# A graph-network layer on one Trainium2 core: ScalarE's PSUM seeds spread over its queue, a bias moved to GpSimd, layer-0 pieces reordered

## The chip, the cores and the metric

The kernel runs on one core of one Trainium2 chip. The metric is the device time of one execution in microseconds; the median of three runs counts.

## What is computed

There are 128 graphs of 64 nodes with 128 features each (`x`) and an adjacency matrix per graph (`adj`, zeros and ones, about one entry in eight set, the diagonal always). A message network runs on every pair of nodes, its output is masked by the adjacency and summed over the neighbours, and an update network adds to the node's features. Cut to what matters, the reference is:

```python
def mlp(x, w0, b0, g0, be0, w1, b1, g1, be1, w2, b2):
    h = layernorm(relu(x @ w0 + b0), g0, be0)
    h = layernorm(relu(h @ w1 + b1), g1, be1)
    return h @ w2 + b2

pair = concat([x_i, x_j])                    # for every i, j of a graph
messages = mlp(pair, msg_...) * adj[..., None]
agg = sum(messages, over j)
out = x + mlp(concat([x, agg]), upd_...)
```

## The kernel before

**Edges in slots.** The kernel does not run all 64 x 64 pairs. For each pair of graphs p (64 of them) it lays the set entries of the adjacency into 640 slots per graph and makes a selection matrix `s` from two halves: `i` (which row a slot belongs to, by way of `d`, `tp` and a cast) and `j` (which column, by a matmul `mk` against `posall` and a comparison with `cmpt`). The halves are written into `s` by DMAs from SyncE's queue. A gather by matmul, `rows` of the graph times `s`, then gives the first layer of the message network for every edge.

**Chunks.** A chunk is 512 slots, four tiles of 128. There are 160 chunks (NCHK), five for two pairs of graphs (QC = 5), ten for a block of four pairs (CPB = 10), 16 blocks. For chunk n the main loop does:

- `layer0(n)` (L553): the gather into one PSUM bank `hps`. A chunk meets one or two graphs' slots, so it is cut into pieces (L544); each piece is two matmuls, one with the low part `abl` of the rows and one with the high part `abh` (L559). ScalarE then writes `h`, relu with bias (L562).
- `stats0` (L564): four transposes into the bank `hT` (L568) and VectorE's statistics (L261), from which a standard deviation `m_sd` per edge follows on ScalarE (L269, `root_of`), once in five chunks.
- `seed(n)` (L595): before the second layer's matmuls are added into PSUM, the bank `z` of the chunk is filled with b1b times the standard deviation of each edge. VectorE does it in one instruction for the four tiles (L601), or ScalarE in four, one per tile, one after the other (L606). `by_vector` (L879) says which: chunks whose number ends in 3, 4 or 8 go to VectorE, the other seven of ten to ScalarE; in the first ten chunks also 1 and 5, and in the last eight every second one.
- `layer1(n)` (L609): eight matmul instructions, two for each tile, that add h times w1c onto the seeded bank (L614), then ScalarE's `y` (L617), and VectorE's statistics of `y` (`stats1`).

There are two `z` banks, for even and odd chunks; each is seeded anew once its last `y` has been read.

**Reductions and updates.** For each pair, GpSimd multiplies weights (L650) and TensorE reduces `y` to a sum per node (L665). For each block of four pairs the update network runs beside the chunks, one small stage at a time: `ysum`, transposes (L711), layers (L725), `layer_out` (L729) with VectorE, copies by ScalarE (L716). Its first bias is `bias0` (L696): m0 = c2u times the degree of a node plus ub0b, four instructions by VectorE for a block of four pairs (L699). The residual `xo` is GpSimd's (L705), as is the scaling `usdb` (L748).

**The order.** The schedule is written by hand. `at(n, place, fn, ...)` (L340) puts a call into a step and a place in it, and the main loop (L1034) goes through the steps n and, in each, through the places in this order: "a", "m", "s", then `layer1(n - L1)` with L1 = 8, then "b", `layer0(n)`, `stats0(n - 1)`, "k", `stats1(n - L1)`, "x", "x1", "x2", "e0", "e1", "e". Each engine runs its instructions in the order in which the program issues them. `seed(n)` is put at step n + L1 - 2, place "x": that is two steps ahead of the chunk's `layer1`, and on ScalarE behind `y` and `h` of that step. `bias0` is at place "m" of a block's step (L821); for the last block at place "e".

Of the kernel before, what the change touches and what calls it, by code (L numbers as in the profile page):

```python
# [14 lines left out]
ALU = mybir.AluOpType  # L15
# [9 lines left out]
def tile_gnn(  # L25
# [40 lines left out]
    nc = tc.nc  # L66
    B, N, C = x.shape
    P = 128
# [8 lines left out]
    CH = 4  # L77
    QC = QT // CH
    NCHK = NQ * QC
    PB = 4  # L80
    NB = NP // PB
    CPB = NCHK // NB
# [92 lines left out]
    W = {}  # L175
# [62 lines left out]
    def bc(t, n, axis=1):  # L238

        s = [P, n, C] if axis == 1 else [P, C, n]  # L240
        return t.unsqueeze(axis).to_broadcast(s)
# [60 lines left out]
    def edge_path(es):  # L302
# [37 lines left out]
        def at(n, place, fn, *args):  # L340
            plan.setdefault((n, place), []).append((fn, args))

        def run(n, place):
            for fn, args in plan.pop((n, place), ()):
                fn(*args)
# [198 lines left out]
        def pieces(n):  # L544

            at_, end = n * CH * P, (n + 1) * CH * P
            while at_ < end:
                g, e = divmod(at_, CAP)
                w = min(end - at_, CAP - e)
                yield g, e, at_ - n * CH * P, w  # L550
                at_ += w

        def layer0(n):  # L553

            ps = ps_h.tile([P, CH * P], F32, name="hps")
            for g, e, c, w in pieces(n):
                s = S[g // 2][:, g % 2, e:e + w]
                for k, ab in enumerate(blocks[g // (2 * PB)]["ab", g // 4 % 2]):
                    nc.tensor.matmul(ps[:, c:c + w], lhsT=ab[:, g % 4, :], rhs=s,  # L559
                                     start=(k == 0), stop=(k == 1))  # L560
            H[n] = hp.tile([P, CH * P], F32, name="h")
            nc.scalar.activation(H[n], ps, AF.Relu, bias=b0c)  # L562

        def stats0(n):  # L564
            q, c = divmod(n, QC)
            ps = ps_t.tile([P, CH, P], F32, name="hT")
            for t in range(CH):
                nc.tensor.transpose(ps[:, t, :], H[n][:, t * P:(t + 1) * P], ident)  # L568
            if c == 0:
                ST0[q] = stp.tile([P, QT // 2, 6], F32, name="st0", bufs=6)  # L570
            for t in range(0, CH, 2):
                two_stats(ST0[q][:, (CH * c + t) // 2, :], ps[:, t:t + 2, :])
# [12 lines left out]
        def z_of(n):  # L585

            if n not in Z:
                Z[n] = zbank(n % 2).rearrange("p (t c) -> p t c", t=CH)
            return Z[n]
# [2 lines left out]
            nc.tensor.matmul(z_of(n), lhsT=slot[:, 0:P], rhs=cmpt[:, 0:CH * C], start=True,  # L592
                             stop=True, skip_group_check=True)

        def seed(n):  # L595

            q, c = divmod(n, QC)
            z = z_of(n)
            k = CH * c
            if by_vector(n):  # L600
                nc.vector.tensor_tensor(  # L601
                    z, bc(W["b1b"], CH),
                    SR[q][:, k:k + CH].unsqueeze(2).to_broadcast([P, CH, C]), op=ALU.mult)
                return
            for t in range(CH):
                nc.scalar.activation(z[:, t, :], W["b1b"], AF.Copy,  # L606
                                     scale=SR[q][:, k + t:k + t + 1])

        def layer1(n):  # L609

            ps = Z.pop(n)
            h = H.pop(n)
            for t in range(CH):
                nc.tensor.matmul(ps[:, t, :], lhsT=h[:, t * P:(t + 1) * P], rhs=W["w1c"],  # L614
                                 start=False, stop=True, skip_group_check=True)
            Y[n] = yp.tile([P, CH, C], F32, name="y")
            nc.scalar.activation(Y[n], ps, AF.Relu)  # L617

        def stats1(n):
            q, c = divmod(n, QC)  # L620
            if c == 0:
                ST1[q] = stp.tile([P, QT // 2, 6], F32, name="st1", bufs=2)
            for t in range(0, CH, 2):
                two_stats(ST1[q][:, (CH * c + t) // 2, :], Y[n][:, t:t + 2, :])
# [58 lines left out]
        def wide(name, u):  # L683

            if name not in u.blk:
                u.blk[name] = updp.tile([P, PB, C], F32, name=name,
                                        bufs=2 if name in ("uo", "xo", "m0") else 1)
            return u.blk[name][:, u.q, :]
# [6 lines left out]

        def bias0(u):  # L696
            u.m0 = wide("m0", u)
            for q in range(u.n):
                nc.vector.scalar_tensor_tensor(  # L699
                    u.m0[:, q, :], W["c2u"], u.blk["deg"][:, u.k0 + q:u.k0 + q + 1], W["ub0b"],  # L700
                    op0=ALU.mult, op1=ALU.add)

        def residual(u):
            u.xo = wide("xo", u)
# [73 lines left out]
        L1 = QC + 3  # L778
# [29 lines left out]
        for b in reversed(range(NB)):  # L808
            o = b * CPB
            n = o + QC + SC  # L810

            if b < NB - 1:
                t = STEADY if b < NB - 3 else LAST[b - NB + 3]
# [6 lines left out]
            for u, n, t, m0_at, xo_at in units:  # L820
                at(n + m0_at, "e" if b == NB - 1 else "m", bias0, u)  # L821
                at(n + xo_at, "e", residual, u)
                at(n + t[0], "a", sums_out, u)
                at(n + t[1], "x", turn, u, "ysum")
                at(n + t[2], "a", turn_out, u, "ysum")
                at(n + t[3], "x", lambda u: layer(u, ("xn", u0a), ("ysumT", W["w2u"])), u)
                at(n + t[4], "m", layer_out, u, "uh", "m0")
                at(n + t[4], "e", upd_m0, u)
                at(n + t[5], "x", turn, u, "uh")
                at(n + t[6], "a", turn_out, u, "uh")  # L830
                at(n + t[7], "a", upd_root0, u)
                if t is STEADY:
                    at(n + t[7], "e", upd_shift, u, 0, PB)
                else:
                    for q0 in range(0, u.n, 2):
                        at(n + t[7], "x", upd_shift, u, q0, q0 + 2)
                at(n + t[8], "x", lambda u: layer(u, ("uhT", W["u1c"])), u)
                at(n + t[9], "m", layer_out, u, "uy", "usdb")
                at(n + t[9], "e", upd_m1, u)
                at(n + t[10], "x", turn, u, "uy")  # L840
                at(n + t[11], "a", turn_out, u, "uy")
                at(n + t[12], "a", upd_root1, u)
                at(n + t[12], "m", upd_inverse, u)
                at(n + t[13], "x", lambda u: layer(u, ("uyT", W["u2c"])), u)
                at(n + t[14], "e" if b == NB - 3 else "m", finish, u)
        for p in range(NP):
            n = p * TG * 2 // CH
# [10 lines left out]
            w = p // 2 * QC + QC + L1 + p % 2  # L858
            last = p // 2 == NQ - 1
            at(w - 4, "a", node_marks, p)  # L860
            q, h = divmod(p, 2)
# [5 lines left out]
        for q in range(NQ):  # L867
            n = q * QC + QC if q else LEAD
# [10 lines left out]
        def by_vector(n):  # L879
            if n >= NCHK - L1:  # L880
                return n % 2 == 1
            return n % CPB in (3, 4, 8) or (n < CPB and n % CPB in (1, 5))

        for n in range(2):
            at(L1 - 1 - n, "s", prime, n)
            at(L1 - 1, "x", seed, n)
        for n in range(2, NCHK):
            at(n + L1 - 2, "x", seed, n)

        warm = ps_y.tile([P, PB, C], F32, name="ys")  # L890

# [50 lines left out]
        compare_here(0, 0)  # L942
        distance(1)
        layer0(0)
        keep_busy(4)
        compare_here(0, 1)
        make_tp(1)
        distance(2)
        marks_here(1)
        layer0(1)  # L950
        keep_busy(4)
        rows_hi(0, 0, 2, 4)
        rows_here(1, 0)
        rows_here(1, 1)
        compare_here(1, 0)
        rows_lo(0, 0, 2, 4)
        layer0(2)
        keep_busy(2)
        make_tp(2)
# [75 lines left out]
        for n in range(last + 1):  # L1035
            run(n, "a")
            run(n, "m")
            if n == NCHK:
                stats0(n - 1)
            run(n, "s")  # L1040
            if 0 <= n - L1 < NCHK:
                layer1(n - L1)
            run(n, "b")
            if n + LEAD < QC or QC <= n < NCHK:
                layer0(n if n >= QC else n + LEAD)
            if n + 1 < QC or QC <= n - 1 < NCHK - 1:
                stats0(n - 1 if n > QC else n + 1)
            run(n, "k")
            if 0 <= n - L1 < NCHK:
                stats1(n - L1)  # L1050
            for k in ("x", "x1", "x2", "e0", "e1", "e"):
                run(n, k)
# [3 lines left out]
    with ExitStack() as es:  # L1056
        es.enter_context(tc.manual_schedule())
        flag = edge_path(es)
# [160 lines left out]
```

## Time and profile before

| | |
|---|---|
| time, median of three runs | 544.2 us (544.17 to 547.51) |
| the profiled execution's own time | 544.21 us |
| its span | 542.4 us |
| granted TensorE clock, mean | 0.996 |
| HBM read and written | 6.82 MB and 4.19 MB |
| L614 on TensorE | 1280 instructions, 280 ns mean |
| L606 on ScalarE, the seeds | 436 instructions, 372 ns mean |
| L601 on VectorE, the seeds | 51 instructions, 682 ns mean |
| L699 on VectorE, the first bias | 64 instructions, 496 ns mean (331 to 886) |
| L705 and L748 on GpSimd, 128 x 512 | 1285 and 1042 ns mean |

How to read it: the span is the time between the first and the last instruction of the profiled execution, and the run's time is 1.8 us more. PE is TensorE's matmuls, PEld its weight loads, DVE is VectorE, ACT ScalarE, POOL GpSimd, and SP SyncE, from whose queue the DMAs start. A line of the order in time has the start, the duration of the merged instructions, the engine, the line of the kernel, the operation, what is written from what, the shape and the count, and in brackets an idle time before it with what ended it. A line of a window has its bounds and length, then the busy time of PE, PEld, DVE, ACT and POOL with the number of instructions, the granted clock, the DMA share and GB/s.

### The profile page before, as it was taken

To read this page: it belongs to the slowest core of one execution; us is meant where nothing else is said; L and a number is where in the kernel's file an instruction comes from. 1 tells how busy PE (TensorE), PEld (TensorE's weight loads), DVE (VectorE), ACT (ScalarE), POOL (GpSimd) and SP (SyncE) were. 2 spreads that over 40 slices of the span, in tenths; PEclk is the share of its full clock that TensorE was granted. 3 is DMA by queue.
4 is the path that set the end of the run, shared out by engine and by line. 5 is a ranking of instruction groups with operands and counts; after the bars stand their busy time and mean duration, and the time that the engine had idled before them with its cause. 6 is when DMAs were issued, how large, how long until landed. Compare 5 with 4: busy or idle time off the path is not lost. (4 is left out here: it accounts for less than half of the span.)

```text
span 542.4 us, 15157 instructions
## 1 busy us (share of the span) xinstructions
PE 520.0 (96%) x5513; PEld 471.6 (87%) x5513; DVE 472.3 (87%) x1271; ACT 475.0 (88%) x1108; POOL 207.4 (38%) x419
## 2 busy tenths in 40 slices
PE   8989999999999999999999999999999999999784
PEld 7777889899898989989898989989999998988764
DVE  6759798998989899898989989898989989896745
ACT  6788999998989999898999989899999989887824
POOL 3103253525334363533435353443536254323230
PEclk9999999999999999999999999999999999999998
DMA  4456666545575665547464554557466445542101
GB/s 99 106 134 117 154 110 149 124 115 121 121 164 101 154 109 128 130 101 166 113 148 96 148 136 98 145 122 147 103 149 129 119 110 117 142 99 32 39 22 43
DMA packets 90762, 63.18 MB, mean 116 GB/s; under 512 B 57398, under 2 KB 74812, under 8 KB 90684
## 3 DMA queue, kind: packets, MB, share of 16 engines
q1 hardware_dynamic: 90396, 62.03, 51.3%
q8 instruction: 46, 0.75, 0.6%
q14 instruction: 32, 0.26, 0.1%
q10 hardware_dynamic: 288, 0.13, 0.1%
HBM read 6.82 MB, written 4.19 MB: 20 GB/s over the span
## 5 line engine op out<-in xcount | busy, mean ns | idle before, releaser
L614 PE MATMUL z<-w1c,h 128*128 128x128 f32 x1280 | 175.8, 280 | 5.2 <-DVE z L601 2.5
L614 PEld LDWEIGHTS z<-w1c,h 128*128 128x128 f32 x1280 | 155.6, 191 | 18.8 <-DVE z L601 8.6
L606 ACT ACTIVATE z<-b1b,m_sd 128x128 f32<-128x128 f32 x436 | 162.1, 372 | 10.7
L261 DVE BATCH_NORM_STATS2 st<-hT 128x6 f32<-128x256 f32 x320 | 118.8, 412 | 20.5 <-PE hT L568 18.3
L261 DVE BATCH_NORM_STATS2 st<-y 128x6 f32<-128x256 f32 x320 | 120.7, 418 | 4.2 <-ACT y L617 4.2
L617 ACT ACTIVATE y<-z 128x512 f32<-128x512 f32 x160 | 94.8, 593 | 20.6 <-PE z L614 19.1
L562 ACT ACTIVATE h<-hps,b0c 128x512 f32<-128x512 f32 x160 | 109.6, 685 | 3.2 <-PE hps L559 3.2
L568 PE MATMUL hT<-ident,h 128*128 128x128 f32 x640 | 97.5, 275 | 2.4 <-DVE st L261 1.3
L559 PE MATMUL hps<-s,abl 128*128 128x512 f32 (+3 forms) x256 | 91.9, 371 | 0.5 <-ACT s L926 0.4
L568 PEld LDWEIGHTS hT<-ident,h 128*128 128x128 f32 x640 | 73.7, 141 | 19.4 <-PE z L614 7.7
L650 POOL TENSOR_TENSOR w<-oh,m_q 128x192 f32<-128x192 f16 x126 | 61.5, 510 | 59.9 <-PE ma L711 25.9
L559 PE MATMUL hps<-s,abh 128*128 128x512 f32 (+3 forms) x256 | 78.0, 323 | 0.0
L517 POOL CAST i<-tp 128x640 fp32r<-128x640 f16 x58 | 41.7, 719 | 93.3 <-issue 47.9
L541 DVE TENSOR_TENSOR j<-mk,cmpt 128x320 fp32r<-128x320 f32 x124 | 58.5, 472 | 1.0 <-PE mk L533 1.0
L502 ACT ACTIVATE d<-slot,mid 128x640 f16<-128x640 f16 x64 | 52.8, 825 | 0.0
L559 PEld LDWEIGHTS hps<-s,abl 128*128 128x128 f32 x256 | 48.9, 191 | 3.6 <-ACT w2cT L200 2.0
L559 PEld LDWEIGHTS hps<-s,abh 128*128 128x128 f32 x256 | 48.9, 191 | 0.1
L665 PE MATMUL ys<-y,w 128*32 128x128 f32 x1488 | 47.0, 275 | 0.0
L665 PEld LDWEIGHTS ys<-y,w 128*32 128x32 f32 x1488 | 38.7, 110 | 4.1 <-issue 3.3
L493 DVE TENSOR_TENSOR abl<-mu,abh 128x512 fp32r<-128x512 f32 (+1 forms) x32 | 21.3, 664 | 22.9 <-ACT abh L487 22.9
L533 PE MATMUL mk<-tp,posall 128*128 128x320 f16 x126 | 37.7, 299 | 0.0
L279 POOL TENSOR_TENSOR m_v<-m_v,st 128x20 f32<-128x20 f32 x31 | 7.7, 250 | 78.3 <-DVE st L261 74.7
(204 smaller groups left out, 841.9 us busy)
## 6 DMA issues: line engine op xcount, KB each, us to landing
s<-i SPq DMA_DIRECT2D x124, 160.0 KB, 2.9
s<-j SPq DMA_DIRECT2D x124, 160.0 KB, 2.7
xn<-in_x_dram SPq DMA_DIRECT2D x15, 256.0 KB, 3.6
out_dram<-uo SPq DMA_DIRECT2D x15, 256.0 KB, 2.9
an<-in_adj_dram SPq DMA_DIRECT2D x16, 128.0 KB, 2.5
oh<-tp SPq DMA_TRANSPOSE x64, 3.3
xn<-in_x_dram SPq DMA_DIRECT2D x2, 128.0 KB
out_dram<-uo SPq DMA_DIRECT2D x2, 128.0 KB, 3.0
```

What stands on the lines that cost most here:

```text
L261: nc.vector.bn_stats(st, src.rearrange("p t c -> p c t"))
L502: nc.scalar.activation(D[p], slot, AF.Abs, bias=blocks[b]["mid"][:, q:q + 1], scale=-1.0)
L517: nc.gpsimd.tensor_copy(IR[p], TP[p])
L541: nc.vector.tensor_tensor(JR[p][:, c], MK.pop((p, k))[:, 0:HC], cmpt[:, c], op=ALU.is_equal)
L559: nc.tensor.matmul(ps[:, c:c + w], lhsT=ab[:, g % 4, :], rhs=s, start=(k == 0), stop=(k == 1))
L562: nc.scalar.activation(H[n], ps, AF.Relu, bias=b0c)
L568: nc.tensor.transpose(ps[:, t, :], H[n][:, t * P:(t + 1) * P], ident)
L606: nc.scalar.activation(z[:, t, :], W["b1b"], AF.Copy, scale=SR[q][:, k + t:k + t + 1])
L614: nc.tensor.matmul(ps[:, t, :], lhsT=h[:, t * P:(t + 1) * P], rhs=W["w1c"], start=False, stop=True, skip_group_check=True)
L617: nc.scalar.activation(Y[n], ps, AF.Relu)
L650: (nc.vector if p == NP - 2 else nc.gpsimd).tensor_tensor(WT[p][:, g], oh, qs, op=ALU.mult)
L665: nc.tensor.matmul(YS[b][g * N + m * HN:g * N + (m + 1) * HN, k, :], lhsT=w[:, g, m, u, :], rhs=y, start=(u == 0), stop=(u == TH - 1), til ...
```

## The change

Four edits. `layer0` runs a chunk's pieces with the widest first. `seed` takes the tiles that it is to write: with none it is VectorE's one instruction, else ScalarE's for those tiles. `by_vector` leaves chunks ending in 4 to ScalarE, so that it has eight of ten. And ScalarE's four seeds of a chunk are put in four places: tile 0 in the new place "y1" of step i = n + L1 - 2, tile 1 in "x" of step i, tile 2 in "y0" and tile 3 in "y2" of step i + 1. The new places run between `layer1` and `layer0` of a step, after "b". Chunk 0 and the last eight chunks keep the four together in "x". `bias0` becomes a multiply and an add by GpSimd over the whole block, in the places where VectorE's four stood.

```diff
         def layer0(n):
             ps = ps_h.tile([P, CH * P], F32, name="hps")
-            for g, e, c, w in pieces(n):
+            for g, e, c, w in sorted(pieces(n), key=lambda v: -v[3]):
...
-        def seed(n):
+        def seed(n, *tiles):
             q, c = divmod(n, QC)
             z = z_of(n)
             k = CH * c
-            if by_vector(n):
+            if not tiles:
                 nc.vector.tensor_tensor(
                     z, bc(W["b1b"], CH),
                     SR[q][:, k:k + CH].unsqueeze(2).to_broadcast([P, CH, C]), op=ALU.mult)
-                return
-            for t in range(CH):
+            for t in tiles:
                 nc.scalar.activation(z[:, t, :], W["b1b"], AF.Copy,
                                      scale=SR[q][:, k + t:k + t + 1])
...
         def bias0(u):
             u.m0 = wide("m0", u)
-            for q in range(u.n):
-                nc.vector.scalar_tensor_tensor(
-                    u.m0[:, q, :], W["c2u"], u.blk["deg"][:, u.k0 + q:u.k0 + q + 1], W["ub0b"],
-                    op0=ALU.mult, op1=ALU.add)
+            deg = u.blk["deg"][:, u.q].unsqueeze(2).to_broadcast([P, u.n, C])
+            nc.gpsimd.tensor_tensor(u.m0, bc(W["c2u"], u.n), deg, op=ALU.mult)
+            nc.gpsimd.tensor_tensor(u.m0, u.m0, bc(W["ub0b"], u.n), op=ALU.add)
...
-            return n % CPB in (3, 4, 8) or (n < CPB and n % CPB in (1, 5))
-
-        for n in range(2):
-            at(L1 - 1 - n, "s", prime, n)
-            at(L1 - 1, "x", seed, n)
-        for n in range(2, NCHK):
-            at(n + L1 - 2, "x", seed, n)
+            return n % CPB in (3, 8) or (n < CPB and n % CPB in (1, 5))
+
+        for n in range(NCHK):
+            if n < 2:
+                at(L1 - 1 - n, "s", prime, n)
+            i = max(n + L1 - 2, L1 - 1)
+            if by_vector(n):
+                at(i, "x", seed, n)
+            elif n >= NCHK - L1 or n == 0:
+                at(i, "x", seed, n, *range(CH))
+            else:
+                at(i, "y1", seed, n, 0)
+                at(i, "x", seed, n, 1)
+                at(i + 1, "y0", seed, n, 2)
+                at(i + 1, "y2", seed, n, 3)
...
             if 0 <= n - L1 < NCHK:
                 layer1(n - L1)
-            run(n, "b")
+            for k in ("b", "y0", "y1", "y2"):
+                run(n, k)
             if n + LEAD < QC or QC <= n < NCHK:
                 layer0(n if n >= QC else n + LEAD)
```

## The prediction

> **What bounds the kernel now.** I read the busy shares first, then the window of the steady part, then the order of time on TensorE and on ScalarE.
>
> ```profile
> PE 520.0 (96%) x5513; PEld 471.6 (87%) x5513; DVE 472.3 (87%) x1271; ACT 475.0 (88%) x1108; POOL 207.4 (38%) x419
> ...
> 90.08:464.31 374.23, 373.57 (x4058) 342.15 (x4057) 346.47 (x923) 347.40 (x807) 161.32 (x312) 1.00 0.57 128
> ```
>
> The second line is the window of chunks 20 to 139, twelve groups of ten: 374.23/12 = 31.19 us a group. TensorE is busy 373.57 of 374.23, VectorE and ScalarE 93%, GpSimd 43%. A chunk's step runs from its first `z` matmul (L614) to the next chunk's. In one group the TensorE lines read:
>
> ```profile
> 313.19 1.16 PE L614 MATMUL z<-w1c,h 128*128 128x128 f32 x8
> ...
> 315.09 1.06 PE L614 MATMUL z<-w1c,h 128*128 128x128 f32 x8
> ...
> 317.07 0.60 PE L711 MATMUL ma<-ident,uh 128*128 128x128 f32 x4
> 317.65 1.16 PE L614 MATMUL z<-w1c,h 128*128 128x128 f32 x8
> ...
> 320.68 1.06 PE L614 MATMUL z<-w1c,h 128*128 128x128 f32 x8
> ...
> 322.62 1.05 PE L614 MATMUL z<-w1c,h 128*128 128x128 f32 x8
> ...
> 327.43 1.16 PE L614 MATMUL z<-w1c,h 128*128 128x128 f32 x8
> ...
> 329.76 0.50 PE L614 MATMUL z<-w1c,h 128*128 128x128 f32 x3
> ```
>
> Named by the last digit of the chunk whose `z` opens them, the steps last: 0: 4.69, 1: 1.90, 2: 2.56, 3: 3.03, 4: 1.94, 5: 4.81, 6: 2.33, 7: 2.70, 8: 3.93, 9: 3.27 us. They are uneven because the reductions and the update's layers sit in some of them. **TensorE's order of work is the bound, and little of the group is waiting.** I find four stops: `z` at 317.65 (four transposes at 0.109 from 317.07 end their issue at 317.51: 0.14), `z` at 301.30 (0.13), and `hT` at 300.12 and 324.26 (0.16 and 0.21 beyond the gap that the same pair of instructions has elsewhere), the first two behind VectorE's seed, the others behind its statistics. A `z` that was waited for also loses 0.10 in its first matmul (0.377 for 0.275). Together 0.14 + 0.13 + 0.16 + 0.21 + 0.20 = 0.84 us of 31.19. No relief of another engine can give more than that.
>
> Now ScalarE in the same place:
>
> ```profile
> 318.84 0.60 ACT L617 ACTIVATE y<-z 128x512 f32<-128x512 f32 x1 [0.55 <-PE z L614]
> ...
> 320.12 1.59 ACT L606 ACTIVATE z<-b1b,m_sd 128x128 f32<-128x128 f32 x4
> 321.78 0.60 ACT L617 ACTIVATE y<-z 128x512 f32<-128x512 f32 x1
> 322.27 0.68 ACT L562 ACTIVATE h<-hps,b0c 128x512 f32<-128x512 f32 x1
> 322.84 1.59 ACT L606 ACTIVATE z<-b1b,m_sd 128x128 f32<-128x128 f32 x4
> ...
> 502.80 1.27 ACT L752 ACTIVATE usdb<-bu1b,um_sd 128x128 f32<-128x128 f32 x4
> ```
>
> The reader is to see two things. First, the seeds at 320.12 stand in step 3 and are chunk 5's: they end at 321.71, and `z` of chunk 5 starts at 322.62, 0.91 later. Those at 322.84, chunk 6's, end 3.0 ahead of 327.43. So seeds are ready well ahead of their `z`. Second, four seeds take 1.59 us. One lasts 0.372, so the distance between them is (1.59 - 0.372)/3 = 0.406: each waits for the one before it to end. The four `usdb` writes, the same instruction into SBUF, take 1.27, a distance of 0.29. [...]
>
> [...] all stops at `z` lie on the first of a chunk's eight matmuls. [...] here L508 lasts 347 to 1112 ns, the long ones beside GpSimd work.
>
> **Part 1, the seeds.** Before, all four of chunk n stood behind `h`, two steps ahead of its `z`. After, tile 0 stands behind `y` and tile 1 behind `h` of that step, and tiles 2 and 3 stand behind the `y` of the next step, which is the last one before their `z`. This makes a loop through TensorE that was not there: `z` of chunk c, `y` of c, the last seeds of c+1, `z` of c+1.
>
> Its length where ScalarE is free: `z` start to `y` start 1.10 (320.68 to 321.78); `y` to the next start 0.48 to 0.49; three seeds (tile 2 of c+1, tile 0 of c+2, tile 3 of c+1) start 0.29 apart, 0.58; the last one 0.37; release to the first matmul 0.06. Sum 2.59. Where chunk c+2 is VectorE's, the middle seed is missing and tile 3 waits for tile 2: 0.405 in place of 0.58. The steps in which c+1 is ScalarE's and TensorE's own work is shorter:
> - step 4: 2.59 for 1.94, +0.65.
> - step 1: `y` starts 1.20 behind `z` (313.19 to 314.39, four small instructions ahead of it); 1.20 + 0.48 + 0.405 + 0.37 + 0.06 = 2.52 for 1.90, +0.62.
> - step 6: an `abh` copy at +0.12, then 0.48 + 0.47 + 0.20, so `y` at 1.27; 2.59 for 2.33, +0.26.
> - step 3 comes to about 2.82 (`m_sd` adds 0.21) of 2.93 and just fits; steps 0, 5, 8 and 9 have room; chunks 3 and 8 are VectorE's.
>
> +1.53, and 3 x 0.10 for first matmuls that waited, +0.30. In step 7 `h` now ends about 3.4 us behind `z`, where the next layer 0 wants its bank at 3.3: +0.15. Sum +1.98 a group.
>
> What it gives: eight chunks at 4 x 0.29 take 9.3 us of ScalarE's queue where seven at 1.53 (322.84 to the next start at 324.37) took 10.7, -1.4 a group. VectorE loses one seed, -0.68 (L601). Neither is the bound, so both count only through the four stops: I take all of them as gone, -0.84.
>
> **Part 2, the first bias.** VectorE loses four L699 (1.82 us of its queue a group). GpSimd gets a multiply like L748 (1.04) and an add like L705 (1.29): 2.33 us a group. They come where GpSimd idled or waited for statistics, and push `m_v` and `posall` back by at most 2.3; `m_v` is wanted two steps on, `posall` at the first mark of step 7, some 3 us later. `m0` is wanted four steps later. So 0; without that cover, 2.3 a group at most. [...] Below zero it gives only what the stops already hold.
>
> **Part 3, the larger piece first.** Only chunks with a 128 and a 384 piece in that order change, two steps a group. In the present order the four matmuls run 318.56 to 319.22, 0.66; a chunk with the large piece first takes 0.61. -0.10 a group; bounds 0 and -0.2.
>
> **Sum.** 1.98 - 0.84 - 0.10 = +1.04 a group, x12 = 12.5. Chunks 10 to 19 (steps of 1.89, 2.05 and 2.34) +1.3; 140 to 149 (1.89, 1.94, 1.90) +1.9; 0 to 9, where VectorE is the bound (19.9 of 20 us from 40 to 60) and loses 0.68 of work against three or four short steps, +0.5. The last eight chunks are seeded as before, and the end after 496 keeps its chain: 0. In all +16.2. The profiled execution is 544.21 (span 542.4 and 1.8 around it), the median 544.2: 560.
>
> **Rivals.**
> - *Each `z` matmul waits for its own tile only* (faster). The fourth tile's matmuls start 0.61 behind the first, so the loop shrinks to about 1.98 and 1.91, just at the shortest steps; it decides below 1.94. Then only -0.94 a group stands: 14 groups, 531. Against it: the bank-wide waits above. 0.09.
> - *The loop is shorter than I reckon*, by 0.3 to 0.4 (seeds closer, `y` earlier): +0.8 in place of +1.98, 0 net: 541 to 548. For it: 0.29 is from SBUF writes. 0.09.
> - *The seeds still stand 0.41 apart, [...]* The first adds 0.23 in step 4, 0.1 in step 3 and late `h`, the second gives back 0.84: +0.5 to 0.85 a group, 567 to 572. 0.20.
> - *Likeliest*, as summed, its own range 551 to 567: 0.62.
>
> A measurement of this kernel can tell about 1% from no change. Faster 0.09, within 1% 0.09, slower 0.82. The range 546 to 574 leaves out the first rival, most of the second and a little at the top, some 0.18.
>
> **What would show it.** The profile after should have steps 4 and 1 at about 2.6 and 2.5 us for 1.94 and 1.90, step 6 near 2.6, and all others as they were or 0.1 shorter; idle of TensorE before L614 put down to ScalarE's `z`, more than 15 us in all; ScalarE and VectorE busy shares lower; L699 gone from VectorE and 2.33 us a group on GpSimd. If steps 1 and 4 stay below 2.1, I am wrong on the loop; if steps 3, 8 or 0 grow, another wait has come.

## The result, and the profile after

The changed kernel takes 560.48 us, the median of four runs (560.23 to 562.53), against 544.22 for the kernel before on the same chip (four runs). The ratio is 1.0292, 95% interval 1.0247 to 1.0337: slower, by 16.3 us. The profiled execution took 562.5 us with a span of 560.4. It is some 2 us longer than the other three, and its first `z` is 2 us later than in the profile before (36.47 for 34.48). These 2 us have nothing to do with the change: they are there at the first layer 0 already (11.34 for 9.28), and in this profile TensorE's full clock is on record from 10.65 us on, for 6.12 before (the same matmul, L473, takes 0.48 us at 9.97 here and 0.32 at 8.21 there). They are left out below.

Line numbers after: seeds L605, `z` L613, `y` L616, first bias L698 and L699. The busy shares:

```profile
PE 525.0 (94%) x5513; PEld 475.8 (85%) x5513; DVE 458.9 (82%) x1192; ACT 470.4 (84%) x1168; POOL 240.2 (43%) x453
```

and the window of chunks 20 to 139, columns as before:

```profile
94.36:481.99 387.63, 375.45 (x4056) 344.74 (x4057) 337.49 (x862) 342.24 (x854) 184.90 (x336) 1.00 0.55 123
```

A group of ten takes 387.63/12 = 32.30 us for 31.19. TensorE's busy time rose by 1.9 us, but the window by 13.4: TensorE, idle for 0.7 us of the window before (374.23 less 373.57), is now idle for 12.2. VectorE and ScalarE are both less busy than before. So none of the engines has become the bound; the order of work between two of them has. The list of waits says which (the columns are: waiting engine, tile and line, releaser, us in all, times, longest):

```profile
PEld z L613 <- ACT z L605: 31.7, 53, 0.9
...
PE z L613 <- ACT z L605: 17.8, 37, 1.1
```

PEld is TensorE's weight loads, which overlap the matmuls (together they are busy for 525.3 us, the matmuls alone for 525.0), so the two lines are not to be added. Before, they came to 4.2 us in 16 waits and 2.5 in 4. The same group of ten as in the prediction, TensorE in order of time:

```profile
325.23 1.16 PE L613 MATMUL z<-w1c,h 128*128 128x128 f32 x8
...
327.75 1.16 PE L613 MATMUL z<-w1c,h 128*128 128x128 f32 x8 [0.45 <-ACT z L605]
...
330.22 1.06 PE L613 MATMUL z<-w1c,h 128*128 128x128 f32 x8
...
333.12 1.12 PE L613 MATMUL z<-w1c,h 128*128 128x128 f32 x8
...
335.77 1.16 PE L613 MATMUL z<-w1c,h 128*128 128x128 f32 x8 [0.46 <-ACT z L605]
...
340.45 1.16 PE L613 MATMUL z<-w1c,h 128*128 128x128 f32 x8
...
343.04 1.16 PE L613 MATMUL z<-w1c,h 128*128 128x128 f32 x8
```

These lines open steps 1 to 7. Steps 1, 4 and 6 last 2.52, 2.65 and 2.59, and the `z` that closes them has the 1.16 us of a `z` that was waited for. Means over twelve groups, in us:

| step | 0 | 1 | 2 | 3 | 4 | 5 | 6 | 7 | 8 | 9 | sum |
|---|---|---|---|---|---|---|---|---|---|---|---|
| before | 4.70 | 1.90 | 2.57 | 3.04 | 1.95 | 4.81 | 2.33 | 2.69 | 3.93 | 3.27 | 31.19 |
| after | 4.71 | 2.51 | 2.48 | 2.91 | 2.63 | 4.69 | 2.59 | 2.47 | 4.04 | 3.27 | 32.30 |

The prediction's lengths of the steps before are up to 0.01 off these means and add up to 31.16, which changes nothing in its sum. What closes step 4 is read on ScalarE:

```profile
334.28 0.60 ACT L616 ACTIVATE y<-z 128x512 f32<-128x512 f32 x1 [0.38 <-PE z L613]
334.77 0.94 ACT L605 ACTIVATE z<-b1b,m_sd 128x128 f32<-128x128 f32 x3
335.65 0.67 ACT L562 ACTIVATE h<-hps,b0c 128x512 f32<-128x512 f32 x1
...
345.83 0.67 ACT L562 ACTIVATE h<-hps,b0c 128x512 f32<-128x512 f32 x1
```

`z` of step 4 starts at 333.12, `y` 1.16 later; 0.49 on, three seeds take 0.94 to 335.71; at 335.77 the next `z` starts. That is the loop, link by link, and ScalarE has waited 0.38 for `y`'s input inside it: each engine waits for the other once a turn. The three seeds start 0.29 apart (334.77, 335.06, 335.35), not 0.406: they go to alternating banks, and in this profile two seeds in a row start 0.29 apart in all 174 pairs that go to different `z` banks, 0.39 to 0.41 in the 47 pairs that go to one. No seed passes the `y` it stands behind: ScalarE's 1167 instructions start in the program's order without exception, as do VectorE's 1185 and GpSimd's 435. The last line belongs to step 8: this `h` ends at 346.50, and layer 0, which writes the bank that it reads, starts behind it at 346.55.

### The profile page after: what moved, and what is told of

It reads as the page before. It is cut to its first block, busy times and chain, and to the rows that moved or that the text cites. A ratio compares the mean times of both kernels' runs of the same rounds, so it can differ in the third digit from the quotient of the medians.

```text
span 560.4 us, 15158 instructions
## 1 busy us (share of the span) xinstructions
PE 525.0 (94%) x5513; PEld 475.8 (85%) x5513; DVE 458.9 (82%) x1192; ACT 470.4 (84%) x1168; POOL 240.2 (43%) x453
## 5 line engine op out<-in xcount | busy, mean ns | idle before, releaser
L613 PE MATMUL z<-w1c,h 128*128 128x128 f32 x1280 | 178.4, 282 | 20.9 <-ACT z L605 17.8
L613 PEld LDWEIGHTS z<-w1c,h 128*128 128x128 f32 x1280 | 155.1, 191 | 40.5 <-ACT z L605 31.7
L605 ACT ACTIVATE z<-b1b,m_sd 128x128 f32<-128x128 f32 x496 | 169.1, 368 | 2.7
L261 DVE BATCH_NORM_STATS2 st<-hT 128x6 f32<-128x256 f32 x320 | 120.5, 418 | 34.6 <-PE hT L568 33.4
L616 ACT ACTIVATE y<-z 128x512 f32<-128x512 f32 x160 | 95.1, 594 | 27.8 <-PE z L613 27.3
L562 ACT ACTIVATE h<-hps,b0c 128x512 f32<-128x512 f32 x160 | 108.0, 675 | 5.1 <-PE hps L559 5.0
L559 PE MATMUL hps<-s,abh 128*128 128x512 f32 (+3 forms) x256 | 74.6, 322 | 0.0
L487 ACT CAST abh<-mu 128x512 fp32r<-128x512 f32 (+1 forms) x32 | 18.3, 572 | 32.3 <-PE mu L475 32.3
```

The costliest lines, as they stand in the source:

```text
L261: nc.vector.bn_stats(st, src.rearrange("p t c -> p c t"))
L605: nc.scalar.activation(z[:, t, :], W["b1b"], AF.Copy, scale=SR[q][:, k + t:k + t + 1])
```

## The experiments

Ratios are to the kernel before on the same chip, whose medians were 544.3 to 545.4.

**Seeds of a chunk together again, the rest of the change kept.** In `after`:

```diff
-                at(i, "y1", seed, n, 0)
-                at(i, "x", seed, n, 1)
-                at(i + 1, "y0", seed, n, 2)
-                at(i + 1, "y2", seed, n, 3)
+                at(i, "x", seed, n, *range(CH))
```

> The changed kernel without the spread: the four seeds of a chunk together behind h, two steps ahead, as before; bias on GpSimd, eight chunks of ten on ScalarE and the larger piece first stay. Loop theory: no loop; but ScalarE's queue holds 8 x 1.53 + 18.2 = 30.4 us in a group of about 30.3 to 31.2, so it is nearly full and little is gained: 538 to 548 us. Rival (the other edits make the loss): 552 to 562 us.

539.63 us, ratio 0.9898 (0.9870 to 0.9926). Steps 4.71, 1.90, 2.57, 3.02, 1.94, 4.61, 2.45, 2.37, 3.87, 3.27, together 30.71. So everything in the change but the spread makes the kernel faster by 1%, and the spread costs 560.5 - 539.6 = 20.9 us.

**The spread alone.** In `before`, `seed(n, *tiles)` and the new places as in the change; chunks, bias and piece order as they were.

> The kernel before with the spread alone: VectorE keeps chunks 3, 4 and 8 and the bias, and the pieces keep their order. Loop theory: the three short steps stay at 2.5 to 2.6 us, since chunks 2, 5 and 7 are ScalarE's here too; VectorE's old stops may stay in part: 558 to 572 us, 562 most likely. Rival (the other edits make the loss): 540 to 548 us.

561.09 us, 1.0313 (1.0285 to 1.0340). Steps 4.71, 2.51, 2.48, 2.93, 2.58, 4.69, 2.59, 2.47, 4.07, 3.27, together 32.31 for 32.30 in `after`. The spread makes the whole of the loss by itself. The relief of VectorE, which gains 4 to 6 us where the seeds are together (the bias and the chunk each alone, below), gains 0.6 beside the spread: TensorE waits for ScalarE, and the step lengths are the same to 0.05 with it and without.

**The dose: the last two seeds behind `h` rather than behind `y`.** In `after`:

```diff
-                at(i + 1, "y0", seed, n, 2)
-                at(i + 1, "y2", seed, n, 3)
+                at(i + 1, "x", seed, n, 2)
+                at(i + 1, "x", seed, n, 3)
```

> The changed kernel with tiles 2 and 3 of each spread seed later still: behind h of the step ahead of their z, one after the other. Loop theory, from the same durations: z to y 1.10, y to its end 0.63 (tile 0 of the next chunk but one waits for it), 0.29, h 0.57, 0.40 between the two tiles, 0.37, 0.06: 3.42 us, 2.98 where the next chunk but one is VectorE's. Steps 4, 1, 6, 3 and 9 of a group become about 3.4, 3.1, 3.15, 3.6 and 3.4 us, +3.9 us a group against the kernel before: 592 to 608 us, 600 most likely. Rival (the loss is not in the loop but in the number of instructions or in contention): 555 to 566 us, as the changed kernel.

604.57 us, 1.1099 (1.1070 to 1.1128). Steps 1, 3, 4, 6 and 9 take 3.09, 3.63, 3.52, 3.17 and 3.42; a group 35.08. The waits grow with the links:

```profile
PEld z L613 <- ACT z L605: 78.2, 79, 1.7
PE z L613 <- ACT z L605: 60.8, 67, 1.4
```

**Late tiles and early tiles exchanged.** If each matmul waited for its own tile, late tiles 2 and 3 would cost less than late tiles 0 and 1, whose matmuls come first. In `after`:

```diff
-                at(i, "y1", seed, n, 0)
-                at(i, "x", seed, n, 1)
-                at(i + 1, "y0", seed, n, 2)
-                at(i + 1, "y2", seed, n, 3)
+                at(i, "y1", seed, n, 2)
+                at(i, "x", seed, n, 3)
+                at(i + 1, "y0", seed, n, 0)
+                at(i + 1, "y2", seed, n, 1)
```

> The changed kernel with the tiles' parts exchanged: tiles 2 and 3 are seeded early, tiles 0 and 1 are the late ones. If TensorE's first matmul on a bank waits for the whole bank (the prediction): the same as the changed kernel, 558 to 563 us. If each tile's matmuls wait for that tile's seed alone, the late tiles are now those that are needed first, some 0.4 us earlier in each of three steps, so 1.2 us a group more: 575 to 580 us.

560.39 us, 1.0290 (1.0268 to 1.0311): to 0.1 us the changed kernel.

```profile
PEld z L613 <- ACT z L605: 31.8, 53, 0.9
```

The same 53 waits and 31.8 for 31.7 us. The first matmul waits for the last seed of the bank, whichever tile it is for. In the traces this wait is one for a semaphore, which the program sets and asks for: in `after` all 125 waits of L613 for ScalarE's stand on the first of a chunk's eight matmuls, and all seeds but one (495 of 496) wait for ScalarE's own. So it is the program that guards the bank as a whole. No run leaves these waits out, so what the bank itself would hold up is not shown.

**The last two seeds ahead of the next `y`.** This takes them out of the loop and leaves them spread. In `after`:

```diff
-                at(i + 1, "y0", seed, n, 2)
-                at(i + 1, "y2", seed, n, 3)
+                at(i + 1, "s", seed, n, 2)
+                at(i + 1, "s", seed, n, 3)
```

> The changed kernel with one thing moved: tiles 2 and 3 of each spread seed stand ahead of the next step's y on ScalarE instead of behind it. Loop theory (the late seeds close a loop z, y, seeds, next z of 2.5 to 2.6 us): the loop is gone, steps ending in 1, 4 and 6 fall back to about 1.9, 1.94 and 2.33 us, most of the four old stops are gone too, so about 0.9 us a group below the kernel before: 528 to 537 us, 531 most likely. Rival (the loss comes from the bias on GpSimd, or from ScalarE having eight of ten chunks): still 552 to 562 us. Second rival (ScalarE is full, so that seeds ahead of y only make y late): 542 to 552 us.

554.45 us, 1.0177 (1.0156 to 1.0198). The expectation missed. Steps 4.70, 1.90, 2.65, 2.94, 2.22, 5.23, 2.33, 2.44, 4.33, 3.27, together 32.02: steps 1 and 6 are back at the values of before, so the loop over `z` is gone, but steps 4, 5 and 8 are longer. TensorE and ScalarE in order of time:

```profile
329.40 1.07 PE L613 MATMUL z<-w1c,h 128*128 128x128 f32 x8
330.84 0.44 PE L559 MATMUL hps<-s,abl 128*128 128x384 f32 x1 [0.36 <-ACT h L562]
```

```profile
329.20 0.58 ACT L616 ACTIVATE y<-z 128x512 f32<-128x512 f32 x1
329.81 0.37 ACT L605 ACTIVATE z<-b1b,m_sd 128x128 f32<-128x128 f32 x1
330.12 0.67 ACT L562 ACTIVATE h<-hps,b0c 128x512 f32<-128x512 f32 x1
```

Two things were missing in my account. The seed between `y` and `h` is tile 0 of the chunk after next, whose bank is the one that this `y` reads: it starts when `y` has ended, 0.61 behind `y`'s start and not 0.49. And `h` is then 0.92 behind `y` where it follows 0.48 to 0.49 behind it without a seed between. Layer 0 has one bank, `hps`, which `h` must have read: there is a second loop, layer 0, `h`, layer 0. With the seeds ahead of `y`, `y` and `h` are later still, and TensorE's weight loads wait 17.8 us for `h` (42 times), against 2.7 (13 times) in the changed kernel.

**Only tile 2 moved ahead.** As above, but tile 3 stays at "y2".

> The changed kernel with tile 2 ahead of the next step's y and tile 3 still behind it: half of the dose. Loop theory: the loop is 1.10 + 0.48 + 0.37 + 0.06 = 2.01 us, 2.11 in the step ending in 1 and 2.18 in the one ending in 6, so steps 1 and 4 of each group take 2.1 and 2.0 us and step 6 its own 2.33; with two first matmuls that waited about 0.47 us a group against 0.94 saved: 534 to 542 us, 537 most likely. Rival (not the loop): as the changed kernel, 552 to 562 us.

553.84 us, 1.0169 (1.0148 to 1.0189): missed, in step 4 for the same reason, by the seed in "y1".

```profile
327.51 0.60 ACT L616 ACTIVATE y<-z 128x512 f32<-128x512 f32 x1
328.15 0.66 ACT L605 ACTIVATE z<-b1b,m_sd 128x128 f32<-128x128 f32 x2
```

The first of the two seeds is the tile 0 that waits for `y`'s end (0.64), tile 3 comes 0.29 behind it. From the `z` at 326.32: 1.19 + 0.64 + 0.66 to the end of tile 3, 0.05 to the next `z` at 328.86, 2.54 in all; the mean of step 4 is 2.54. In steps 1 and 6 the missing link is tile 2 itself: ahead of `y`, it puts `y` at 1.34 and 1.57 behind `z`, for 1.20 and 1.28 in the changed kernel. Reckoned again with the queue as it is, the loop gives 2.25 in step 1 (2.24 measured) and 2.48 in step 6 (2.48). The loop's rule holds; I had left links out.

**The three other edits, each alone, in `before`.** The bias on GpSimd; `by_vector` with (3, 8); the larger piece first.

> The kernel before with the first bias on GpSimd alone. It takes 1.8 us a group from VectorE's queue, whose lateness makes the four stops of TensorE (0.84 us a group at most): 533 to 542 us, 538 most likely. Rival (the stops are behind the chunk 4 seed, not the bias): 542 to 546 us. Rival (GpSimd's 2.3 us hold up VectorE's two-input work): 545 to 552 us.

540.37 us, 0.9917 (0.9896 to 0.9938), a group 30.77. Steps 7 and 8 are shorter (2.37 and 3.83), the rest as before.

> The kernel before with one edit: chunks ending in 4 are seeded by ScalarE, four together behind h. It takes 0.68 us a group from VectorE, so the stop at hT in step 5 (0.21) and perhaps the one at z in step 3 go; ScalarE's queue is then nearly full (30.4 of 31 us) and may make y and h late. Expected 541 to 545 us. If ScalarE is the bound at once: 546 to 552 us.

539.44 us, 0.9894 (0.9864 to 0.9923), a group 30.79. Steps 5 and 7 are shorter (4.60 and 2.39), step 6 is longer (2.45 for 2.33). The expectation missed: it is better than expected.

> The kernel before with one edit: the larger piece of a chunk first. The prediction has 0.10 us a group, 0.05 in each of two steps: 542.5 to 543.5 us. By the steps of the versions with and without it (3.83 and 3.81, 3.04 and 3.02) it is 0.04 a group: 543.5 to 544.2 us, not to be told from none.

545.06 us, 0.9990 (0.9979 to 1.0000), not to be told from no change. Steps 3 and 8 are 0.02 shorter each, step 5 is 0.04 longer; a group takes 31.16.

> The kernel before with the bias on GpSimd and the larger piece first; seeds and chunks as before, so ScalarE keeps seven of ten. If ScalarE's full queue (eight of ten at 1.53 us) held back the version with the seeds together, this one is faster than its 539.6: 532 to 538 us. If relief of VectorE by the chunk 4 seed is what removes the stops, it is slower than that: 540 to 544 us.

Bias and order together: 539.33 us, 0.9895 (0.9868 to 0.9923), a group 30.75. It lies between the two expectations and doesn't decide between them. With the eighth chunk as well it is the kernel with the seeds together, at 539.63 and 30.71 a group. So bias and chunk do not add: alone they gain 0.42 and 0.40 us a group, together with the order 0.48. What they share is step 7, which each of them shortens by 0.30 to 0.32 by itself; the bias's 0.10 of step 8 and the chunk's 0.21 of step 5, which costs 0.12 in step 6, are their own. The 0.14 of step 2 is in none of them gone (2.57). The step lengths are the surer measure here, since the clock alone moves the time by 1.6 us (last section).

**A spread that stays off the loop.** From the kernel with the seeds together, up to three of a chunk's four seeds go behind ScalarE's copies at the start of the next step, one behind each copy, and so ahead of that step's `y`, with other work between two writes to one bank. Chunks ending in 2 or 7 and the first twenty keep four together.

```diff
-                at(i, "x", seed, n, *range(CH))
+                later.append((n, i))
+        for n, i in later:
+            after = plan.get((i + 1, "a"), [])
+            k = 0
+            if n >= 2 * CPB and n % CPB not in (2, 7):
+                k = min(len([v for v in after if v[0] not in QUIET]), CH - 1)
+            at(i, "x", seed, n, *range(CH - k))
...
```

> The version with the seeds together (eight chunks of ten on ScalarE, bias on GpSimd, larger piece first), but with up to three of a chunk's four seeds put between the copies that ScalarE makes ahead of the next step's y, where there are such copies (steps 0, 3, 5 and 8 of a group): the spacing without the loop. Loop theory: no new stop, some 0.11 us of ScalarE's queue saved for each seed put apart, about 0.55 us a group, of which part reaches TensorE: 533 to 539 us, 537 most likely. If any seed placed later than h of its own step costs TensorE time: 541 us and more.

534.60 us, 0.9806 (0.9781 to 0.9831): better than both kernels. ScalarE in order of time:

```profile
302.82 0.77 ACT L605 ACTIVATE z<-b1b,m_sd 128x128 f32<-128x128 f32 x2
303.53 0.58 ACT L465 COPY xnT<-ma 128x512 f32<-128x512 f32 x1
304.01 0.37 ACT L605 ACTIVATE z<-b1b,m_sd 128x128 f32<-128x128 f32 x1
304.31 0.82 ACT L502 ACTIVATE d<-slot,mid 128x640 f16<-128x640 f16 x1
305.03 0.35 ACT L605 ACTIVATE z<-b1b,m_sd 128x128 f32<-128x128 f32 x1
305.32 0.58 ACT L616 ACTIVATE y<-z 128x512 f32<-128x512 f32 x1
```

The two seeds between copies take 0.30 and 0.29 of the queue (304.01 to 304.31, 305.03 to 305.32); of the two that stand together the first takes 0.40. With the seeds together ScalarE was busy for 357.92 of 368.49 us, 97%, the most loaded engine behind TensorE; here for 353.37 of 365.94:

```profile
90.07:456.01 365.94, 365.94 (x4058) 342.51 (x4057) 333.00 (x863) 353.37 (x855) 186.51 (x336) 1.00 0.58 131
```

A group takes 30.50 for 30.71, step 6 being back at 2.33. Of the 5.0 us, 2.6 come from this window and 2.4 from the steps of chunks 147 and 148 (4.10 and 3.67 for 4.91 and 5.26), told in the last section; 1.6 of these 2.4 are the clock's, so some 3.4 us are the spread's.

> The kernel before with the spacing between copies alone; the bias and chunks 3, 4 and 8 stay with VectorE, the pieces keep their order. The four stops of the kernel before lie behind VectorE, and ScalarE has room, so by the loop theory the spacing alone gives almost nothing: 542 to 545 us. If ScalarE's time counts by itself: 538 to 541 us.

The same spread in `before`, nothing else changed: 543.11 us, 0.9973 (0.9956 to 0.9990). A group takes 31.16 for 31.19. Where ScalarE is 93% busy and the stops lie behind VectorE, a shorter ScalarE queue gains little, as expected; 0.8 us of what it does gain is the step of chunk 147 (4.12 for 4.91).

## Why the prediction was right

It was 560.0 us, and 560.5 was measured. The mechanism is shown, and it is the loop. That the sum came within 0.5 us is in part luck: some terms were off by up to about 1 us of the run, and nearly cancelled.

- **The loop of part 1.** Steps 1, 4 and 6 were put at 2.52, 2.59 and 2.59; they are 2.51, 2.63 and 2.59. Step 4 is longer in nine of the twelve groups (2.64 to 2.65), where its `z` had itself half waited (1.12 us) and `y` came 1.16 behind it, not 1.10; in the other three `y` comes at 1.10 to 1.11 and the step takes 2.59 to 2.60. Step 3 "just fits" with 2.82 of 2.93: it is 2.91. The loop's cause is shown by the seeds put together (gone), by the spread alone (whole), and by the dose (longer by the links added).
- **The wait for the bank.** That TensorE's first matmul waits for all four tiles, on which the loop rests, is shown by the exchange of tiles, 560.39 us against 560.48. By the traces the waits are for semaphores of the program, which guards the bank as a whole. The rival in which each matmul waits for its tile only is out.
- **Seeds 0.29 or 0.41 apart.** In the changed kernel, 0.29 where banks alternate and 0.39 to 0.41 where two of one bank follow; both as used.
- **Layer 0 waiting for `h` in step 8.** Predicted 0.15. In the profile layer 0 starts at 346.55; a `z` of 1.06 us is followed by layer 0 at +0.81 elsewhere, here that is 345.51 + 0.81 = 346.32; so 0.23. It was mis-sized because of the tile 0 that waits for `y`'s end (345.52, behind a `y` from 344.90: 0.62), which the account of part 1 did not have. The same link was what made two expectations miss.
- **The stops, -0.84 taken as all gone.** In the changed kernel they are: step 2 loses 0.14 and gains the 0.10 of a `z` that was waited for (2.48 measured, 2.53 by this sum), step 3 loses 0.10 (2.91 measured, 2.94), step 5 loses 0.21 and gains 0.10 (4.69, 4.70), step 7 loses 0.13 and 0.16 and gains 0.10 (2.47, 2.50), step 8 loses 0.10 and gains 0.23 (4.04, 4.06). But the reason given was not all of it. The spread alone, without either relief of VectorE, shows the same step lengths within 0.05; and with the reliefs and the seeds together step 2's stop stays. The longer steps 1, 4 and 6 cover the stops whatever VectorE saves.
- **Part 3, -0.10.** It is -0.03 a group by the step lengths (-0.02 in each of two steps was there, but step 5 grew), and not to be told from nothing by the time.
- **Part 2, nothing by itself.** In `before`, moving the bias gains 0.42 a group, all of it from stops of TensorE (steps 7 and 8), as said. Beside GpSimd's adds L451 takes half of the relief back (1334 ns for 410), see the last section; whether the gain would be larger without that is not shown.
- **Outside the window.** The windows differ by 0.8 in chunks 0 to 9 (predicted 0.5), 1.5 in 10 to 19 (1.3), 13.4 in the twelve groups (12.5), 1.2 in 140 to 149 (1.9), and -0.9 behind them (0): 16.0, for a predicted 16.2. In 140 to 149 steps 1, 4 and 6 are longer by 0.62, 0.71 and 0.69 as reckoned, but step 7 is shorter, 4.23 for 4.91: TensorE's transposes of `uy` wait 1.12 us there for ScalarE's copy of `ysumT`, and waited 1.91 before; the spread alone has 1.12 too. Behind them the step of chunk 150 is 3.97 for 4.44. It is 3.99 with the seeds together and 3.97 with the bias alone, but 4.44 with the chunk alone, so the moved bias gives these 0.47; the other 0.4 lie behind chunk 159, where the profiles differ by as much from one to the next.

What stays open: why the stop of step 2 stays with either relief of VectorE and with both, why that of step 5 goes with the chunk and not with the bias, and where the small differences of chunks 0 to 19 come from.

## What to carry to other kernels

Instructions that are ready well ahead of their use may be free where they stand and costly one step later (20.9 us here): draw the loop that the moved instruction closes through the engine that sets the pace, add its links from the trace with the real neighbours in its engine's queue, and compare the sum with each step's own length, short steps first. Spacing the writes to one PSUM bank (0.29 for 0.405 us each) paid here only with independent work between them that stands ahead of the loop's instructions, and only where ScalarE was nearly full (97%, not 93%). Two reliefs of one engine do not add where they remove the same stops, so measure each edit alone and then without the others.

## What the runs showed of the hardware that was not expected

VectorE's L451, an instruction with two inputs from SBUF that the change doesn't touch, went from a median of 410 ns to 1334. GpSimd and VectorE in order of time in the changed kernel:

```profile
335.81 1.04 POOL L698 TENSOR_TENSOR m<-c2u,deg 128x512 f32<-128x512 f32 x1
336.93 1.28 POOL L699 TENSOR_TENSOR m<-m,ub0b 128x512 f32<-128x512 f32 x1
```

```profile
337.15 1.35 DVE L451 SCALAR_TENSOR_TENSOR a<-an 128x256 f32<-128x256 f32 x1
```

It starts 0.22 into the bias's add and ends (338.50) only when that has ended (338.21). With the bias alone moved the median is 1346 ns too; in the five kernels whose bias stays with VectorE it is 405 to 410. The difference, 0.92 us a group, is half of the 1.82 that the moved bias had taken from VectorE. The prediction had seen such a slowing for `tp` (L508) only: in the profile before its 64 instructions take 347 to 389 ns, but for 14 of 721 to 1112 that stand beside GpSimd's L444 or L748. What the two engines contend for is not shown.

The second concerns the clock. In chunk 147 of the kernel with the seeds together, TensorE waits once for ScalarE, and its granted clock halves afterwards. TensorE in order of time, then three windows:

```profile
483.49 0.66 PE L709 MATMUL ma<-ident,uy 128*128 128x128 f32 x4 [1.91 <-ACT ysumT L714]
```

```profile
480.58:483.49 2.91, 1.00 (x10) 0.76 (x8) 2.28 (x7) 2.76 (x7) 1.76 (x4) 1.00 0.00 0
...
484.70:488.10 3.40, 3.40 (x18) 3.40 (x17) 0.75 (x3) 2.44 (x7) 2.65 (x4) 0.50 0.00 0
488.10:490.00 1.90, 1.90 (x19) 1.90 (x18) 1.01 (x4) 0.50 (x2) 0.00 (x0) 1.00 0.00 0
```

1.00 us of work in 2.91, and from 1.2 us after the wait the clock is 0.50 for 3.4 us; the step of chunk 148 takes 5.26 for 3.67, 1.6 us of the run. The profiles with the bias alone, the order alone, and both have it too, behind waits of 1.92, 1.89 and 1.91; those of the kernel before and of the chunk alone, with 1.91 both, do not: four of six, so a wait of this size is followed by the half clock at some times only. In the eight profiles in which the wait is 0.94 to 1.14 (all those with seeds spread or between copies) the clock stays at 1.00 there.

The clock's own record says more on when. In all fourteen traces it changes only at whole multiples of 3.413 us after its first rise: before and after have one such change, 532.48 and 546.13 us behind that rise, 156 and 160 times 3.413; in the one above they are at 140, 141 and 155 times. So how this grid lies to the wait may matter. In the stretch of the grid just ahead of the drop, 481.25 to 484.66 above, TensorE was busy for 1.50 of 3.41 us, a share of 0.44, and for 1.50 to 1.52, 0.44 to 0.45, in the other three. In the kernel before, with the same wait, the lowest stretch there has 1.72 us, 0.50, and no drop follows; with the shorter waits none there is under 0.67. The share is not all: with the chunk alone a stretch has 1.54 us, 0.45, and the clock stays, and a stretch of 0.47 near 26 us (1.61 us in the profile before) is followed by a drop in two profiles (the bias alone, the seeds between copies in `before`) and by none in five others. What decides is not shown.
